# State-space scans with interleaved convolution layers on one core: decays computed three states ahead, statistics deferred behind the next product

## The chip, the cores and the metric

The kernel runs on one core of one Trainium2 chip. A core has five engines that each work through their own queue in order: TensorE (PE in the profile; PEld are its weight loads), VectorE (DVE), ScalarE (ACT), GpSimd (POOL) and SyncE (SP), which here only issues DMA transfers. They meet through semaphores. The metric is the device time of one execution in microseconds (us); the time before is the median of three runs.

## The reference, cut to what matters

The input x is 16 images of 192 channels of 64 x 64. Four layers follow, each `x = x + layer(group_norm(x))`:

- layer 0: a small per-channel network (1-3-3-3-1, with tanh) at x - 0.5 and x + 0.5, then the absolute difference of two sigmoids;
- layer 1: a linear map over the channels of a pixel and its four neighbours;
- layer 2: a selective scan, which takes most of the time (below);
- layer 3: depthwise 3x3, 5x5, 1x7 and 7x1 convolutions, a pointwise convolution, a batch norm over all images, a clip to [0, 6].

```python
# layer 2: K = 4 directions, N = 16 states, L = 4096 positions
xs = jnp.stack([xf, xt, xf[..., ::-1], xt[..., ::-1]], axis=1)   # rows, columns, both backward
dts, Bs, Cs = jnp.split(jnp.einsum('bkdl,kcd->bkcl', xs, x_proj_weight), [R, R + N], axis=2)
delta = softplus(einsum('bkrl,kdr->bkdl', dts, dt_projs_weight) + dt_projs_bias)
A = -exp(A_logs)
def step(h, inp):
    d, u, Bt, Ct = inp
    dA = exp(d[..., None] * A)
    h = dA * h + (d * u)[..., None] * Bt[:, :, None, :]
    return (h, einsum('bkdn,bkn->bkd', h, Ct))
```

The sums over n are added over the four directions, with a skip term. The group norms need the mean and variance of each layer's input: these are the statistics of which the change speaks.

## The kernel before

**Tiling.** Images are worked in 8 pairs; a pair's 2 x 192 channels make three blocks j of 128 partitions. For one pair `scans` (L761) does layer 2 and `layer3` (L1018) layer 3. The layers 0 and 1 and the projections that feed layer 2 are the generator `front` (L359); while pair i is scanned, the front of pair i + 1 is worked a little at a time between the scan's steps. The front of the first pair runs alone ahead of everything, with three interleaved streams of layer 0 (`deep`). The eighth pair has no front beside it.

**A scan step.** `todo` holds 48 tiles (j, direction, chunk of 1024 positions), each with 16 states n: 768 steps s a pair, 6144 in all. A step takes

- `load_c` (L829): SP loads a row of C, broadcast to 128 partitions, into `cb` (4 buffers), two steps ahead;
- `spread` (L875): two matmuls put B of state n on all partitions, into PSUM `pbt` (2 buffers), two steps ahead;
- `decay` (L868): ScalarE makes `dA = exp(delta * a)`, into `dA` (2 buffers), two steps ahead;
- `product` (L888): VectorE multiplies `pbt` by `du` in place;
- `scan` (L891): VectorE's scan `h = dA * h + pbt` along the positions (8 buffers `h`), then ScalarE's copy of the last column into `state`, then GpSimd's `h * cb`, and for every fourth step a DMA that adds one `h` to another;
- `add_up` (L909): TensorE sums the `h` of a tile in PSUM `ysum`, four steps behind; ScalarE copies the result to `X` or `Xt` (L939).

At n = 3 of each tile `step_rest` (L845) makes the next tile's `delta` by a softplus, for which ScalarE loads another table, and loads it back for the next decay.

**What sets the order.** Inside `scans` every engine call is kept in the order in which the program makes it (`_InOrder`, L54). So the loop at L970 is the order by hand: `load_c(s + 2)`, `product(s)`, `scan(s)`, `decay(s + 2)`, `spread(s + 2)`, then the parts of n = 3 and 8, then one slot of the front, then `add_up(s - 4)`. During layer 0 a step has one slot of the front, at n = 0 two and at n = 3 and 5 none (L1003); elsewhere about one, two where n is a multiple of 4, and matmuls of layer 1 count as half a slot.

**Statistics on VectorE.** `bn_stats` works on 512 columns (0.67 to 0.69 us each). It stands in the front for the input (L385, two a slot), for the result of layer 0 (L490, in `tail`, L464) and of layer 1 (L626, in `done`, L620), and in `finish` (L941) for X, the sum of both scan orientations, when a block j is done. `finish` adds `Xt` to `X` on GpSimd (on VectorE for the last block) in four chunks, one a step from n = 5, with the statistics of each chunk one step later. Since slots come after `scan(s)`, all these statistics stand behind a scan and ahead of the next product.

**Layer 0's order.** A chunk of x is 128 x 512; it has four units q of four slots each. `tail` goes on by one yield a slot: GpSimd and ScalarE turn the network's output into a likelihood, GpSimd adds it to x (L487), and two yields later come the statistics and the store of x (L490, L491). The load of the chunk two ahead (L548) stands in the second slot of q = 3 and takes the buffer (of 3) that the tail has just left. `norm` (L427) of the next chunk is in the second slot of q = 1.

Of the kernel before, what the change touches and what calls it, by code (L numbers as in the profile page):

```python
# [11 lines left out]
F32 = mybir.dt.float32  # L12
# [10 lines left out]
P = 128  # L23
# [45 lines left out]
class _Engines:  # L69
# [3 lines left out]
    def __init__(self, tc, in_order):  # L73
        nc = tc.nc
        of = (lambda e: _InOrder(tc, e)) if in_order else (lambda e: e)
        self.pe, self.act, self.dve = of(nc.tensor), of(nc.scalar), of(nc.vector)
        self.gps, self.sp = of(nc.gpsimd), of(nc.sync)
        self._in_order, self._table = in_order, None

    def table(self, *names):  # L80
# [11 lines left out]
def conv_preact_kernel(ctx: ExitStack, tc: tile.TileContext, a: dict):  # L92
# [266 lines left out]
    def front(i, o, E, ps, deep):  # L359

        with tc.tile_pool(name="f_st", bufs=1) as stat:
# [4 lines left out]
            with tc.tile_pool(name="f0", bufs=3) as pool:  # L366
# [12 lines left out]
                for u in range(4 * NT):  # L379
                    yield  # L380
                    load(u + 2)
                    j, c = divmod(u, 4)
                    x = got.pop(u)
                    for h in range(2):
                        E.dve.bn_stats(sts[0][:, j, 2 * c + h, :], x[:, 512 * h : 512 * h + 512])  # L385
            yield
# [11 lines left out]
    def layer0(i, E, ps, deep, st, gm, rstd):  # L398
        with tc.tile_pool(name="l0w", bufs=1) as w_, tc.tile_pool(name="l0x", bufs=3) as xk, tc.tile_pool(
# [11 lines left out]
            def stream(chunks, no):  # L411
# [52 lines left out]
                def tail(ci):  # L464
# [21 lines left out]
                    E.gps.tensor_scalar(sg, sg, 1e-6, None, ALU.max)  # L486
                    E.gps.tensor_tensor(x, x, sg, ALU.add)  # L487
                    yield
                    yield
                    E.dve.bn_stats(st[:, j, c, :], x)  # L490
                    E.sp.dma_start(out=row_tiles(x1_d)[:, j, 512 * c : 512 * c + 512], in_=x)  # L491

# [34 lines left out]
                for u, (ci, q) in enumerate(units):  # L527
# [17 lines left out]
                    if q == 1:  # L545
                        norm(at + 1)
                    if q == 3:
                        load(at + 2)  # L548
                        xns.pop(ci)
                    yield "l0"  # L550

                    for s in (1, 0):
# [3 lines left out]
                        first(u + 1, s)  # L556
                        tanh(t2[:, s, :], ba[s][:GR], 2, g, s)
                        yield "l0"
                    before = ci, q, g, ba, t2
# [19 lines left out]
    def layer1(o, E, ps, deep, st, gm, rstd):  # L579
        with tc.tile_pool(name="l1w", bufs=1) as w_, tc.tile_pool(name="l1x", bufs=2) as xk, tc.tile_pool(  # L580
# [39 lines left out]
            def done(c, jo, p):  # L620
# [4 lines left out]
                yield  # L625
                E.dve.bn_stats(st[:, jo, c, :], x)  # L626
                E.sp.dma_start(out=row_tiles(o.x2)[:, jo, 512 * c : 512 * c + 512], in_=x)

            def advance():
# [131 lines left out]
    def scans(i, o, st3, nxt):  # L761

        E = _Engines(tc, True)
        with ExitStack() as es:
# [5 lines left out]
            two = pool("l2two", 2)  # L770
            hp = pool("l2h", 8)
            cp = pool("l2c", 4)
            sp_ = pool("l2s", 3)
# [94 lines left out]
            def decay(s):  # L868
                t, n = divmod(s, N)
                j, k, at, first = todo[t]  # L870
                dA = dAs[s] = two.tile([P, LC], F32, name="dA")
                E.table(TANH)
                E.act.activation(dA, made[t][0], AF.Exp, scale=a_neg[:, k, j, n : n + 1])
# [67 lines left out]
            def finish(j):  # L941

                for c in range(4):
# [5 lines left out]
                    yield  # L949
                    for h in range(2 * c, 2 * c + 2):  # L950
                        E.dve.bn_stats(st3[:, j, h, :], X[:, 512 * h : 512 * h + 512])
                yield
# [6 lines left out]
            for _ in step_rest(0):  # L959
                pass  # L960
            load_dt(1)
            for s in range(2):
                load_c(s)
                decay(s)
                spread(s)
# [4 lines left out]
            for s in range(total):  # L970
# [8 lines left out]
                if n == 6:  # L979
                    load_xc(t + 1)  # L980
                product(s)
                scan(s)
                if s + 2 < total:
                    decay(s + 2)
                    spread(s + 2)
# [16 lines left out]
                if kind == "l0":  # L1002
                    for _ in range({0: 2, 3: 0, 5: 0}.get(n, 1)):  # L1003
                        kind = next(fr, None) if kind == "l0" else kind
                elif n not in (3, 5):
                    done = 0
# [7 lines left out]
            for g in (finish(NT - 1), fr):  # L1014
                for _ in g:
                    pass

# [286 lines left out]
```

## Time and profile before

| what | value |
|---|---|
| median of 3 runs | 28522.85 us (28516.71 to 28527.12) |
| the profiled execution: its own time | 28505.5 us |
| its span, first to last instruction | 28503.4 us |
| VectorE busy | 24241.3 us (85%) |
| TensorE busy / weight loads | 23450.2 us (82%) / 9578.6 us (34%) |
| GpSimd busy | 20851.6 us (73%) |
| ScalarE busy | 16193.3 us (57%) |
| DMA | 191 GB/s on the mean |
| granted TensorE clock | 0.909 on the mean |
| scans (VectorE), 6144 | 2.35 us each with a state, 2.29 without |
| products (VectorE), 6144 | 1.21 us each |
| decays (ScalarE), 6144 | 1.15 us each |
| h times cb (GpSimd), 6144 | 2.45 us each |

Busy is the time in which an engine has an instruction in work. Idle time of an engine is listed with what ended it, which is inferred from the semaphores: `DVE h L64 <- ACT dA L64` is VectorE's scan (it writes `h`) that waits for ScalarE's decay. L64 is the line of the recording helper, so instructions inside `scans` are told apart by their tiles, not by their lines. A few of VectorE's waits are large but lie outside the scans: `fst L490` and `l_xr L624` in the first pair's front, `l_p` in layer 3, `rl` in the last pass.

### The profile page before, as it was taken

To read this page: it belongs to the slowest core of one execution; us is meant where nothing else is said; L and a number is where in the kernel's file an instruction comes from. 1 tells how busy PE (TensorE), PEld (TensorE's weight loads), DVE (VectorE), ACT (ScalarE), POOL (GpSimd) and SP (SyncE) were. 2 spreads that over 40 slices of the span, in tenths; PEclk is the share of its full clock that TensorE was granted. 3 is DMA by queue.
4 is the path that set the end of the run, shared out by engine and by line. 5 is a ranking of instruction groups with operands and counts; after the bars stand their busy time and mean duration, and the time that the engine had idled before them with its cause. 6 is when DMAs were issued, how large, how long until landed. Compare 5 with 4: busy or idle time off the path is not lost. (4 is left out here: it accounts for less than half of the span.)

```text
span 28503.4 us, 207850 instructions
## 1 busy us (share of the span) xinstructions
PE 23450.2 (82%) x57140; PEld 9578.6 (34%) x57140; DVE 24241.3 (85%) x15397; ACT 16193.3 (57%) x23037; POOL 20851.6 (73%) x10440
## 2 busy tenths in 40 slices
PE   8799977999689987899879997799968998766663
PEld 4333323333233332333323332333323333222221
DVE  0388988899889988989888898888988988899994
ACT  7377445774467643775447744577445764344443
POOL 2388876887768876788768887688776887777772
PEclk9899988999899998999889998899989999888886
DMA  4478864887568974788747887478855887467765
GB/s 101 133 215 214 213 200 137 215 211 214 162 175 220 215 214 118 215 214 216 210 124 214 215 214 205 132 216 213 216 170 166 217 210 218 121 187 190 190 184 234
DMA packets 2007999, 5447.98 MB, mean 191 GB/s; under 512 B 550392, under 2 KB 550616, under 8 KB 1989424
## 3 DMA queue, kind: packets, MB, share of 16 engines
q1 hardware_dynamic: 1782192, 4578.95, 55.6%
q0 software_dynamic: 221184, 805.40, 14.9%
q10 hardware_dynamic: 3456, 50.33, 0.4%
q8 instruction: 455, 7.45, 0.1%
q14 instruction: 712, 5.83, 0.1%
HBM read 3896.19 MB, written 329.51 MB: 148 GB/s over the span
## 5 line engine op out<-in xcount | busy, mean ns | idle before, releaser
L64 POOL TENSOR_TENSOR h<-h,cb 128x1024 f32<-128x1024 f32 x6144 | 14820.0, 2447 | 4719.8 <-ACT state L64 4189.9
L64 DVE TENSOR_TENSOR_SCAN h<-dA,state,pbt 128x1024 f32<-128x1024 f32 x4608 | 10813.8, 2347 | 1135.7 <-ACT dA L64 614.9
L64 PE MATMUL ysum<-h,ident 128*128 128x512 f32 x18432 | 9406.9, 635 | 45.8 <-DMA h<-h 45.5
L64 DVE TENSOR_TENSOR pbt<-du,pbt 128x1024 f32<-128x1024 f32 x6144 | 7429.5, 1209 | 377.1 <-PE pbt L64 341.4
L64 ACT ACTIVATE dA<-delta,t_alog 128x1024 f32<-128x1024 f32 x6144 | 7035.5, 1146 | 6.6
L64 PEld LDWEIGHTS ysum<-h,ident 128*128 128x128 f32 x18432 | 3764.6, 205 | 4305.5 <-issue 3922.7
L64 ACT COPY state<-h 128x1 f32<-128x1 f32 x6144 | 1150.0, 187 | 6955.5 <-DVE h L64 6903.8
L64 PE MATMUL pbt<-bp,pick 96*128 96x512 bf16 x8192 | 2716.5, 416 | 2246.5 <-DVE h L64 2216.1
L64 DVE TENSOR_TENSOR_SCAN h<-dA,pbt 128x1024 f32<-128x1024 f32 x1536 | 3512.4, 2287 | 362.7 <-ACT dA L64 152.8
L64 PE MATMUL p<-t,wts 96*128 96x512 f32 x5376 | 2741.3, 610 | 136.0 <-ACT t L64 136.0
L64 PE MATMUL p<-m,wms 128*96 128x512 f32 (+1 forms) x5376 | 2724.3, 609 | 10.5 <-ACT lu L64 10.0
L64 ACT ACTIVATE t<-p,bias 96x512 f32<-96x512 f32 x2688 | 1814.2, 680 | 1104.1 <-PE p L64 1095.4
L64 PEld LDWEIGHTS <-pick 96*128 96x128 bf16 x8192 | 692.3, 101 | 5114.8 <-DVE h L64 3431.4
L1071 POOL TENSOR_TENSOR l_g<-l_g,l_m 128x1024 f32<-128x1024 f32 x672 | 1614.8, 2405 | 454.8 <-ACT l_g L1067 348.2
L64 PE MATMUL l_p<-l_xp,w1s 128*128 128x512 f32 x3920 | 1851.4, 604 | 7.0 <-POOL l_xp L64 7.0
L64 PE MATMUL pbt<-bp,pick_mix 96*128 96x512 bf16 x4096 | 1307.4, 402 | 634.0 <-DVE h L64 620.2
L1094 DVE SCALAR_TENSOR_TENSOR l_p<-xp,wc,l_p 128x1024 f32<-128x1024 f32 x1248 | 1589.6, 1287 | 257.4 <-PE l_p L1088 226.5
L64 POOL DMA_DIRECT2D h<-h x1536 | 1355.0, 882 | 494.9 <-POOL h L64 426.3
L1076 PE MATMUL l_p<-xp,diag 128*128 128x512 f32 x2688 | 1286.0, 637 | 333.0 <-DVE l_y L1094 281.2
L64 PEld LDWEIGHTS p<-t,wts 96*128 96x128 f32 x5376 | 1024.6, 193 | 1295.7 <-issue 882.7
L64 ACT ACT_TABLE_LOAD x1104 | 1416.4, 1283 | 19.5
L64 POOL TENSOR_TENSOR du<-delta,xn 128x1024 f32<-128x1024 f32 x384 | 1022.7, 2663 | 451.4 <-ACT delta L64 451.4
(219 smaller groups left out, 17750.1 us busy)
## 6 DMA issues: line engine op xcount, KB each, us to landing
cb<-cp_d SPq DMA_DIRECT2D x2048, 512.0 KB
cb<-c_d SPq DMA_DIRECT2D x2048, 512.0 KB
h<-h POOLq DMA_DIRECT2D x1536, 512.0 KB, 6.9
cb<-cp_d SPq DMA_DIRECT2D x2048, 256.0 KB
cb<-c_d SPq DMA_DIRECT2D x2048, 256.0 KB
m<-l_xn SPq DMA_DIRECT2D x3072, 128.0 KB
bp<-bp_d SPq DMA_DIRECT2D x384, 192.0 KB
f0x<-in_x SPq DMA_DIRECT2D x96, 512.0 KB
```

Of the source, the lines that this page charges most:

```text
L64: return self._tc.keep_in_program_order(call(*args, **kw))
L1071: nc.gpsimd.tensor_tensor(g, g, m, ALU.add)
L1076: nc.tensor.matmul(ps[:, cs], diag[:, j, t, :], window(j, 16 * c + 8 * h, 8, tap), start=(t == 0), stop=False,)
L1094: nc.vector.scalar_tensor_tensor(image(y if tap is TAPS[-1] else ps), window(j, 16 * c, 16, tap), factor(j, tap), image(ps), ALU.mult, ALU ...
```

## The change

Two things change, both in the order of the program.

1. `dA` gets a pool of its own with three buffers, and decays are issued three steps ahead: decay(s + 3) where decay(s + 2) stood. Spreads and loads of C stay two ahead.
2. Statistics of the in-order front and of `finish` are not issued at once but collected (`later`) and issued by `between`, which the loop calls after `product(s)` and ahead of `scan(s)`; in layer 0's slots of n = 0 and n = 12 it is also called directly behind the slot. The tails of layer 0 and layer 1 get a yield: layer 0's statistics and store come three yields after the addition instead of two, and both tails end one yield later. `finish` has two yields a chunk instead of one. Layer 0's load of the chunk two ahead goes from the second slot of q = 3 to the fourth. In the first pair's front and in layer 3, which are not kept in order, `later` issues at once.

No computation is added or taken away.

```diff
+    def later(self, call):
+        if self._in_order:
+            self._later.append(call)
+        else:
+            call()
+
+    def between(self):
+        for call in self._later:
+            call()
+        self._later.clear()
...
                     x = got.pop(u)
-                    for h in range(2):
-                        E.dve.bn_stats(sts[0][:, j, 2 * c + h, :], x[:, 512 * h : 512 * h + 512])
+                    def stats(x=x, j=j, c=c):
+                        for h in range(2):
+                            E.dve.bn_stats(
+                                sts[0][:, j, 2 * c + h, :], x[:, 512 * h : 512 * h + 512]
+                            )
+                    E.later(stats)
...
                     E.gps.tensor_tensor(x, x, sg, ALU.add)
-                    yield
-                    yield
-                    E.dve.bn_stats(st[:, j, c, :], x)
+                    for _ in range(3):
+                        yield
+                    E.later(lambda: E.dve.bn_stats(st[:, j, c, :], x))
                     E.sp.dma_start(out=row_tiles(x1_d)[:, j, 512 * c : 512 * c + 512], in_=x)
+                    yield
...
                     if q == 1:
                         norm(at + 1)
-                    if q == 3:
-                        load(at + 2)
-                        xns.pop(ci)
                     yield "l0"
...
                         tanh(t2[:, s, :], ba[s][:GR], 2, g, s)
+                        if q == 3 and s == 0:
+                            load(at + 2)
+                            xns.pop(ci)
                         yield "l0"
...
-                E.dve.bn_stats(st[:, jo, c, :], x)
+                E.later(lambda: E.dve.bn_stats(st[:, jo, c, :], x))
                 E.sp.dma_start(out=row_tiles(o.x2)[:, jo, 512 * c : 512 * c + 512], in_=x)
+                yield
...
+            da = pool("l2a", 3)
...
-                dA = dAs[s] = two.tile([P, LC], F32, name="dA")
+                dA = dAs[s] = da.tile([P, LC], F32, name="dA")
...
                     yield
-                    for h in range(2 * c, 2 * c + 2):
-                        E.dve.bn_stats(st3[:, j, h, :], X[:, 512 * h : 512 * h + 512])
+                    yield
+                    def stats(c=c):
+                        for h in range(2 * c, 2 * c + 2):
+                            E.dve.bn_stats(st3[:, j, h, :], X[:, 512 * h : 512 * h + 512])
+                    E.later(stats)
...
+            for s in range(3):
+                decay(s)
             for s in range(2):
                 load_c(s)
-                decay(s)
                 spread(s)
...
                 product(s)
+                E.between()
                 scan(s)
+                if s + 3 < total:
+                    decay(s + 3)
                 if s + 2 < total:
-                    decay(s + 2)
                     spread(s + 2)
...
                         kind = next(fr, None) if kind == "l0" else kind
+                        if n in (0, 12):
+                            E.between()
...
             for g in (finish(NT - 1), fr):
                 for _ in g:
-                    pass
+                    E.between()
+            E.between()
```

More of the change, by code (lines that the diff above doesn't have):

```diff
@@ L77, in __init__ @@
         self.gps, self.sp = of(nc.gpsimd), of(nc.sync)
+        self._later = []
         self._in_order, self._table = in_order, None
+    def later(self, call):
[7 more added lines that the diff above has]
+        self._later.clear()
     def table(self, *names):
@@ L487, in tail @@
                     E.gps.tensor_tensor(x, x, sg, ALU.add)
+                    for _ in range(3):
+                        yield
+                    E.later(lambda: E.dve.bn_stats(st[:, j, c, :], x))
+                    E.sp.dma_start(out=row_tiles(x1_d)[:, j, 512 * c : 512 * c + 512], in_=x)
                     yield
-                    yield
-                    E.dve.bn_stats(st[:, j, c, :], x)
-                    E.sp.dma_start(out=row_tiles(x1_d)[:, j, 512 * c : 512 * c + 512], in_=x)
                 def advance():
```

## The prediction

> **What bounds the kernel now.** I read the page's shares first: VectorE is busy 24241.3 us of a 28503.4 us span and has the largest share, so what counts is the 4262 us in which it idles. Then the windows of two pairs of images, from the first scan to the last: the seventh, which carries the front (layers 0, 1 and the projections) of the next pair in its slots, and the eighth, which carries none. Columns: window, length, busy time of PE, PEld, DVE, ACT, POOL, granted clock, DMA share, GB/s.
>
> ```profile
> 21577.20:24615.00 3037.80, 2633.98 (x6528) 1079.29 (x6528) 2754.52 (x1681) 1888.02 (x2753) 2375.91 (x1187) 0.93 0.80 211
> 24974.80:27775.00 2800.20, 1928.03 (x4204) 716.39 (x4204) 2671.57 (x1553) 1166.65 (x1722) 2119.53 (x1014) 0.83 0.69 189
> ```
>
> VectorE paces both: idle 283.3 us with a front, 128.6 without. So a front causes 154.7 us of idling a pair, 1083 us over the seven pairs that have one: a ceiling for a change that only removes idle time. Next, VectorE's waits (total us, times, longest), the rows that lie in the scans:
>
> ```profile
> DVE h L64 <- ACT dA L64: 767.7, 937, 4.5
> ...
> DVE pbt L64 <- PE pbt L64: 341.4, 428, 5.9
> ...
> DVE fst L64 <- POOL l_x L64: 125.3, 71, 4.2
> ...
> DVE st L64 <- POOL X L64: 103.3, 57, 5.6
> ```
>
> The first row is scans waiting for their decay; the third and fourth are statistics waiting for GpSimd; the second is products waiting for TensorE's spread, which the change does not touch. The timelines of VectorE and ScalarE around step n=3 of a tile of 16 steps show how a decay comes late (start, length, instruction, idle time):
>
> ```profile
> 12295.57 1.21 DVE L64 TENSOR_TENSOR pbt<-du,pbt 128x1024 f32<-128x1024 f32 x1
> 12296.88 2.35 DVE L64 TENSOR_TENSOR_SCAN h<-dA,state,pbt 128x1024 f32<-128x1024 f32 x1
> 12299.14 1.21 DVE L64 TENSOR_TENSOR pbt<-du,pbt 128x1024 f32<-128x1024 f32 x1
> 12301.99 2.35 DVE L64 TENSOR_TENSOR_SCAN h<-dA,state,pbt 128x1024 f32<-128x1024 f32 x1 [1.64 <-ACT dA L64]
> ```
>
> ```profile
> 12295.92 1.01 ACT L64 COPY X<-ysum 128x1024 f32<-128x1024 f32 x1 [1.92 <-PE ysum L64]
> 12296.95 1.28 ACT L64 ACT_TABLE_LOAD   x1
> 12298.25 1.11 ACT L64 ACTIVATE delta<-v,t_dtb 128x1024 f32<-128x1024 f32 x1
> 12299.26 0.18 ACT L64 COPY state<-h 128x1 f32<-128x1 f32 x1
> 12299.46 1.28 ACT L64 ACT_TABLE_LOAD   x1
> 12300.76 1.15 ACT L64 ACTIVATE dA<-delta,t_alog 128x1024 f32<-128x1024 f32 x1
> ```
>
> Product to scan is 1.31 us from start to start, scan to product 2.26: a step of 3.57. The scan at 12301.99 is n=6; it could have begun at 12299.14 + 1.31 = 12300.45. Its decay waited on ScalarE behind the copy of the sums, the softplus and two table loads.
>
> **Part A, decays three ahead.** No instruction is added. Each decay moves one step forward in ScalarE's order and still waits, through the state copy ahead of it, for the scan that frees its buffer. So decay s now ends where decay s-1 ended, and its slack grows by 3.57. Before, it had 1.31 + 2.26 + 1.31 = 4.88 us from the end of scan s-2, and needs 0.19 + 1.15, so a ScalarE lag over 3.5 us showed; after, over 7.1.
> The 767.7 us are not all real. In 513 waits the scan starts within 0.13 us of its own decay's end and more than 0.06 us past the nominal 1.31; they hold 709 us. The rest are gaps of about 0.2 us with the decay long done, at one scan in four, which waits for four semaphores; they stay.
> Not all of the 709 is won. Spreads stay two ahead in two PSUM buffers, in TensorE's queue behind matmuls that need ScalarE's tanh, so a late ScalarE also makes the next spreads late. At 12801.58 a scan (n=3) starts 3.21 us late for a decay; the spread two steps on ends at about 12807.6, and its product starts there: that wait would only move. I therefore bounded each of the 513 waits by the smallest spare time (product's start less the end of its spread) of the steps behind it, up to the first spread that began within 0.25 us of the scan that released it, since from there TensorE follows VectorE. Whole trace, by position, waits / covered in us: n=6 379.0 / 270.6; n=3 97.9 / 25.1; n=7 64.8 / 60.4; n=4 44.7 / 7.4; n=11 31.2 / 31.2; n=15 28.2 / 0.9; n=5 23.2 / 0.5; the others 40.2 / 16.0. Sum 709 / 412. I take **412**; ends 271 (n=6 alone) and 709 (TensorE's queue moves forward too). What is late next is the spread.
>
> **Part B, statistics a slot later.** Layer 0's wait for x (125.3 us, longest 4.2): the statistics come a slot later and mostly behind one more product, 3.57 + 1.2 = 4.8 us, beyond the longest wait. 28 of 168 stay directly behind a scan, so **115**; ends 0 and 125. The statistics of X (103.3 us): their additions go from steps 5, 6, 7, 8 to 5, 7, 9, 11 and the statistics to 8, 10, 12, 14, so 8.4 us instead of 3.6 behind the addition; but in those tiles GpSimd is nearly as full as VectorE (59.5 and 60.4 us busy in the tile from 12405 to 12480), so it may not catch up: **60**; ends 0 and 103.
>
> **Part C, statistics between a product and its scan.** This row shows both effects:
>
> ```profile
> 12278.43 2.35 DVE L64 TENSOR_TENSOR_SCAN h<-dA,state,pbt 128x1024 f32<-128x1024 f32 x1
> 12280.70 0.67 DVE L64 BATCH_NORM_STATS2 fst<-l_x 128x6 f32<-128x512 f32 x1
> 12281.28 1.21 DVE L64 TENSOR_TENSOR pbt<-du,pbt 128x1024 f32<-128x1024 f32 x1
> 12282.59 2.35 DVE L64 TENSOR_TENSOR_SCAN h<-dA,state,pbt 128x1024 f32<-128x1024 f32 x1
> ```
>
> Instructions that don't depend on each other start 0.08 to 0.09 us before the one ahead ends (scan to statistics 2.27 for 2.35, statistics to product 0.58 for 0.67); scan on product, which depends, starts 0.10 after its end. No row has statistics straight behind a product they don't need; by the others it would be 1.21 - 0.09 = 1.12, then 0.60 to the scan: 1.72 where now 0.60 + 1.31 = 1.91 are spent. In the changed order 442 groups stand so (168 of layer 1, 140 of layer 0, 70 of the input, 64 of X): 442 x 0.19 = **84**; ends 44 (the 0.10 gap alone) and 84. No product behind statistics has under 0.65 us to spare on its spread, so 0.6 us earlier costs none of them a wait.
> [...]
>
> **What else moves.** Layer 0's load of x goes two slots later, still six slots (over 20 us) ahead of its normalisation; nothing of VectorE waits for it now. On SP it no longer stands right behind the store of the same buffer, where SP waited 650.6 us for landings; the broadcast rows (cb) queue behind it, but only GpSimd waits for them (187.7 us with c_d), which is not the bound: 0. Stores of x come a slot later too: 0. Layer 0 gets one slot longer; the front is done some seven tiles ahead of the pair's end, which covers 3.6 us. The first front is scheduled freely and only its load and tail move: 0, at worst one of its slots, about 6 us.
>
> **The sum.** 412 + 115 + 60 + 84 = 671 us. The profiled execution took 28505.5 (span 28503.4), which gives 27834; it lies 17 us under the median of the runs, 28522.85, so on that scale **27850**. All high ends: 709 + 125 + 103 + 84 = 1021, or 27500, close to the ceiling of 1083. All low ends: 271 + 44 = 315, or 28210.
>
> **Rivals.**
> 1. *The spread takes over (18%).* ScalarE's lag stays what it is, so TensorE's queue is late in more places, and GpSimd's statistics waits return where VectorE runs ahead. For it: products already wait 341.4 us for spreads. Against: at n=6, over half of the waits, the spare time is there. Only the low ends remain: about 28210.
> 2. *TensorE's queue moves forward too (10%).* My spare times treat a spread that is behind tanh as fixed; if it gains with VectorE, nearly every wait goes: about 27500.
> 3. *TensorE becomes the bound by its clock (6%), slower than before.* In a tile with layer 0 its records cover 58 of some 61 us, and a matmul that takes 0.59 at full clock takes 1.06 at the lower one. If denser work lowered the granted clock, 0.93 in the seventh pair, its 2634 us of a pair would stretch by 2634 x (0.93 / c - 1). With half of the stretch falling through to VectorE, the gain of 96 us a pair is eaten at c = 0.87; at 0.85 it is 124 a pair, 28 x 7 = 200 us slower, 28720. Against: the eighth pair has less matmul work and a lower clock, 0.83.
> 4. *It does nothing (4%):* decays would still end late because each waits for the scan that frees its buffer. Against: that scan is now three back. 28520.
>
> **Chances.** The forecast has 62%, the rivals 18, 10, 6 and 4. Faster by over 0.2%, about what a measurement of this kernel can tell from no change: 0.62 + 0.18 + 0.10 = 0.90; the same 0.04; slower 0.06. The range takes in rivals 1 and 2 with the ends of the unknown costs: 27480 to 28230.
>
> **What would show it.** Right for A: scans' wait for dA falls from 768 to below 300 us, nothing left at n=6, and products' wait for pbt grows from 341 to some 600. Right for B: both statistics rows below 60 us together. Right for C: product to scan 1.7 us where statistics stand between. Wrong: waits for dA as before (A does nothing), the pbt row above 900 (rival 1), or a granted clock below 0.87 in the pairs with a front (rival 3). The eighth pair should hardly change, 2800 us.

## The result, and the profile after

Median of 4 runs 28274.64 us (28253.27 to 28295.17), the kernel before beside it 28519.78 (28509.89 to 28527.12): ratio **0.9914**, 95% interval 0.9897 to 0.9931. Faster by 245 us, where 671 were forecast; the time lies just above the range, whose upper end was 28230. The profiled execution took 28295.17, its span is 28293.1 and its mean clock 0.904 (before 0.909).

The windows of the seventh and eighth pair, first scan to last, columns as before:

```profile
21391.40:24394.70 3003.30, 2639.30 (x6528) 1088.12 (x6528) 2751.99 (x1681) 1873.26 (x2754) 2374.57 (x1189) 0.93 0.81 214
24764.20:27554.60 2790.40, 1931.18 (x4204) 718.63 (x4204) 2670.79 (x1553) 1165.90 (x1722) 2119.14 (x1016) 0.83 0.69 190
```

VectorE's busy time is within 3 us of before in both pairs. The pair with a front lost 34.5 us (3037.8 to 3003.3), the one without 9.8. The granted clock of these two windows is 0.93 and 0.83, to two digits as before. VectorE's waits (total us, times, longest):

```profile
DVE pbt L64 <- PE pbt L64: 812.1, 862, 9.7
...
DVE h L64 <- ACT dA L64: 116.8, 512, 2.3
DVE st L64 <- POOL X L64: 115.6, 44, 4.1
...
DVE fst L64 <- POOL l_x L64: 3.6, 7, 0.5
```

Scans hardly wait for late decays any more (767.7 to 116.8, and 476 of the 512 waits left are gaps of at most 0.3 us), nor statistics for x (125.3 to 3.6). But products wait 812.1 us for spreads where 341.4 stood and some 600 were expected, and the statistics of X wait no less than they did (103.3 to 115.6). The step that the prediction showed, scan n=6 of the same tile, now looks so; first VectorE, then ScalarE, then TensorE:

```profile
12193.02 2.35 DVE L64 TENSOR_TENSOR_SCAN h<-dA,state,pbt 128x1024 f32<-128x1024 f32 x1
12195.73 1.23 DVE L64 TENSOR_TENSOR pbt<-du,pbt 128x1024 f32<-128x1024 f32 x1 [0.37 <-PE pbt L64]
12197.17 2.35 DVE L64 TENSOR_TENSOR_SCAN h<-dA,state,pbt 128x1024 f32<-128x1024 f32 x1 [0.20 <-DVE pbt L64]
```

```profile
12192.65 1.01 ACT L64 COPY X<-ysum 128x1024 f32<-128x1024 f32 x1 [1.92 <-PE ysum L64]
```

```profile
12193.71 1.13 PE L64 MATMUL v<-dt,t_dtw 12*128 12x512 f32 x4 [1.10 <-ACT X L64]
12194.77 0.92 PE L64 MATMUL pbt<-bp,pick 96*128 96x512 bf16 x2
12195.49 3.30 PE L64 MATMUL p<-m,wms 128*96 128x512 f32 x4
```

The scan that stood 1.64 us for its decay has it in time. Now its product stands 0.37 for the spread, which stands in TensorE's queue behind the matmuls of `v`; these need the PSUM banks of `ysum`, and so ScalarE's copy of the sums. Here 1.64 became 0.57 (0.37 and 0.20).

Part C did what it was to do. VectorE with a statistic between product and scan:

```profile
12239.68 1.21 DVE L64 TENSOR_TENSOR pbt<-du,pbt 128x1024 f32<-128x1024 f32 x1
12240.80 0.68 DVE L64 BATCH_NORM_STATS2 fst<-l_x 128x6 f32<-128x512 f32 x1
12242.17 2.35 DVE L64 TENSOR_TENSOR_SCAN h<-dA,state,pbt 128x1024 f32<-128x1024 f32 x1 [0.68 <-DMA h<-h]
```

The statistic starts 1.12 after the product, as worked out (this scan then waits for another thing). Over the trace, with layer 0's 140: product to statistic 1.116, statistic to scan 0.600, together 1.716 in the median. Before, a statistic of layer 0 and then product to scan took 1.90 in the median of the 97 groups in which nothing waited (0.585 and 1.315), so the place is worth 0.185 us, as forecast. The Trainium skill's page "VectorE: DVE Perf Modes", section "The DRAIN you can't avoid", says that an instruction does not start until the pipe is empty behind the one ahead, and adds that one that is not held starts earlier. This trace agrees with the addition: the statistic, which needs nothing of the product, starts 0.09 us before the product's end (1.12 for 1.21).

### The profile page after: what moved, and what is told of

It reads as the page before. It is cut to its first block, busy times and chain, and to the rows that moved or that the text cites. A ratio compares the mean times of both kernels' runs of the same rounds, so it can differ in the third digit from the quotient of the medians.

```text
span 28293.1 us, 208020 instructions
## 1 busy us (share of the span) xinstructions
PE 23483.5 (83%) x57140; PEld 9639.0 (34%) x57140; DVE 24223.9 (86%) x15397; ACT 16092.7 (57%) x23037; POOL 20787.2 (73%) x10440
## 5 line engine op out<-in xcount | busy, mean ns | idle before, releaser
L64 DVE TENSOR_TENSOR pbt<-du,pbt 128x1024 f32<-128x1024 f32 x6144 | 7441.2, 1211 | 852.4 <-PE pbt L64 812.1
```

Source lines behind the costliest of these rows:

```text
L64: return self._tc.keep_in_program_order(call(*args, **kw))
```

## The experiments: what each part is worth

Each kernel's ratio is against runs of the kernel before on the same chip (median 28528 to 28536; 28520 beside the changed kernel), with its interval; differences between kernels are those of their medians, unless a ratio is named. Where the chips differ, so can the medians by these 16 us. Three theories were open when the first four ran: Q, that a late ScalarE makes TensorE's queue late and so the spreads; S, that the statistics' new place holds back what follows the scan; G, that GpSimd's lag reaches the spreads by way of the sums of h.

**e1, the decays alone.** The kernel before, `dA` in its own pool of three, decays three ahead.

```diff
+            da = pool("l2a", 3)
...
-                dA = dAs[s] = two.tile([P, LC], F32, name="dA")
+                dA = dAs[s] = da.tile([P, LC], F32, name="dA")
...
+                if s + 3 < total:
+                    decay(s + 3)
                 if s + 2 < total:
-                    decay(s + 2)
                     spread(s + 2)
```

> The kernel before with part A alone: three buffers for dA and decays three ahead, statistics where they were. Theory Q (a late ScalarE makes TensorE's queue late through the tanh and the copy of the sums, so the spread takes over the wait): scans' wait for dA under 150 us, products' wait for pbt from 341 to 650 or more, the time 150 to 300 us under before, so 28220 to 28370. Rival S (the statistics' new place in front of the scan holds back the scan's followers and eats part A's gain): part A alone wins over 400 us, under 28120. Rival G (GpSimd's lag, through the sums of h, is what makes the spreads late): as Q in time, but TensorE's idle ahead of late spreads is put down to h and its DMA.

28525.07, ratio 0.9994 (0.9986 to 1.0003): no gain at all, where Q expected at least 150 us and S over 400. The rows are Q's: scans' wait for decays 767.7 to 125.4, products' for spreads 341.4 to 705.0. And the statistics of x wait 240.0 instead of 125.3; that such waits return where VectorE runs ahead stood in the prediction's first rival.

**e2, the statistics alone** (the changed kernel, decays two ahead, the pool with two buffers).

```diff
-            da = pool("l2a", 3)
+            da = pool("l2a", 2)
...
-                if s + 3 < total:
-                    decay(s + 3)
+                if s + 2 < total:
+                    decay(s + 2)
                 if s + 2 < total:
```

> The changed kernel without part A: two buffers for dA, decays two ahead; statistics deferred, a slot later, load of x later. Theory Q: the waits for GpSimd's x (125 us) go, product to scan with statistics between is 0.19 us shorter in 442 places, but VectorE meets the decays earlier: 50 to 200 us under before, 28320 to 28470, with scans' wait for dA above 768. Rival S: no gain or slower, 28500 or more.

28422.67, ratio 0.9958 (0.9945 to 0.9970). Spreads 343.6, decays 837.4: the spreads get late only with part A, and the statistics alone win time, so S falls.

**e3, part C alone** (e2 without the added slots of part B).

```diff
-                    for _ in range(3):
+                    for _ in range(2):
                         yield
                     E.later(lambda: E.dve.bn_stats(st[:, j, c, :], x))
...
-                    yield
                     def stats(c=c):
```

> Part C alone: statistics between product and scan, with layer 0's and X's statistics at the old number of yields and decays two ahead (layer 0's load of x stays at its later place, the end of the tails too). Theory Q: 30 to 90 us under before, 28430 to 28490; the difference to the run with deferred statistics a slot later is what the later slot (part B) is worth. If the pipe empties whatever the order, part C is worth nothing: within 30 us of before, if GpSimd's waits are as before.

28433.85, ratio 0.9965 (0.9951 to 0.9978): all but some 11 us of e2. A statistic behind the next product is already 1.2 us later: the wait for x falls from 125.3 to 69.5 by that alone. Part B's added slots (e3 to e2) take another 69 us from x's row and 10 from X's, yet they are worth only those 11 us: scans wait longer for decays instead, first e3, then e2.

```profile
DVE h L64 <- ACT dA L64: 774.5, 941, 3.9
```

```profile
DVE h L64 <- ACT dA L64: 837.4, 939, 9.2
```

In all three one row had grown that has nothing to do with scans: VectorE's additions of X at the end of a pair waited 119 us for ScalarE's copy, for 54.9 before. The gaps between the last scan of one pair and the first of the next had gone from 2519.9 to 2565.0 us in all (after against before). GpSimd shows why; before, then after, at the end of the same pair:

```profile
14433.36 1.20 POOL L1040 TENSOR_SCALAR diag<-ident,wc 128x128 f32<-128x128 f32 x2 [1.09 <-DVE h L64]
14434.53 2.35 POOL L64 TENSOR_TENSOR h<-h,cb 128x1024 f32<-128x1024 f32 x1
```

```profile
14296.73 8.72 POOL L1073 TENSOR_SCALAR diag<-ident,wc 128x128 f32<-128x128 f32 x15
14305.42 2.34 POOL L64 TENSOR_TENSOR h<-h,cb 128x1024 f32<-128x1024 f32 x1
```

The instructions that build layer 3's weights are not kept in order. With the new pool 15 of them, not 2, stand ahead of the pair's last `h * cb`, on which its last sums, the copy of X and layer 3 wait. Two kernels test it.

**e5, the changed kernel with the old pool.**

```diff
-            da = pool("l2a", 3)
...
-                dA = dAs[s] = da.tile([P, LC], F32, name="dA")
+                dA = dAs[s] = two.tile([P, LC], F32, name="dA", bufs=3)
```

> The changed kernel whole, but the three decay buffers taken from the pool that held the two before (bufs=3 on that one tile) instead of from a pool of their own. Theory P (the new pool costs time between pairs): with the pool, 15 of the 21 instructions that build layer 3's diagonal weights stand ahead of GpSimd's last product h x cb of each pair; with the old pool 2 do. 13 x 0.6 us = 7.8 us later for the last sums, of which 6.4 us a pair showed (gaps between pairs 2565 us in all against 2520 before, end 738 against 728), so this kernel should take 55 us less than the changed one, about 28220, with VectorE's wait for ScalarE's X at the pair's end back from 119 to some 55 us. Rival: the gaps grew because the additions of X and their statistics come later; then nothing changes, 28275. The waits within the scans (decay 117, spread 812) should be as in the changed kernel by both.

**e6, the kernel before with the pool alone.**

```diff
+            da = pool("l2a", 2)
...
-                dA = dAs[s] = two.tile([P, LC], F32, name="dA")
+                dA = dAs[s] = da.tile([P, LC], F32, name="dA")
```

> The kernel before, with nothing changed but that its two decay buffers come from a pool of their own. Theory P: 50 to 55 us slower than before, about 28585, gaps between pairs 2565 instead of 2520, the wait for ScalarE's X 119 instead of 55, and every wait within the scans as before (decay 768, spread 341). Rival: no difference, 28530.

e5: 28208.34, ratio 0.9886 (0.9873 to 0.9900), 66 us under the changed kernel. e6: 28606.62, ratio 1.0025 (1.0015 to 1.0035), 71 us over the kernel before. The additions' wait for X in e5 and in e6 (54.9 before, 118.8 in the changed kernel):

```profile
DVE X L64 <- ACT X L64: 54.5, 8, 6.8
```

```profile
DVE X L64 <- ACT X L64: 119.4, 8, 15.0
```

The pool's price is shown from both sides; the gaps between pairs sum to 2507.1 and 2569.0 us.

**e15, the decays alone in the old pool** (the kernel before).

```diff
-                dA = dAs[s] = two.tile([P, LC], F32, name="dA")
+                dA = dAs[s] = two.tile([P, LC], F32, name="dA", bufs=3)
...
+                if s + 3 < total:
+                    decay(s + 3)
                 if s + 2 < total:
-                    decay(s + 2)
                     spread(s + 2)
```

> The kernel before with the decays three ahead alone, in the old pool: e1 without the pool's price of 67 to 71 us. By theory P 28455 (e1 28525 less 70), so that this part is worth some 75 us in place of the 412 forecast; the decays' row falls to about 125 and the spreads' grows to about 705, as in e1. If it stays at 28520, the pool's price is not what hid this part in e1.

28452.72, ratio 0.9971 (0.9960 to 0.9983): 76 us, as expected. VectorE's waits in it:

```profile
DVE pbt L64 <- PE pbt L64: 764.2, 754, 7.8
...
DVE fst L64 <- POOL l_x L64: 252.3, 110, 4.5
...
DVE h L64 <- ACT dA L64: 125.8, 526, 1.1
DVE h L64 <- DVE pbt L64: 123.0, 592, 0.6
...
DVE h L64 <- ACT state L64: 35.8, 93, 2.9
```

Two rows of the kernel before that were not shown yet:

```profile
DVE h L64 <- ACT state L64: 120.4, 153, 4.3
...
DVE h L64 <- DVE pbt L64: 69.2, 335, 0.6
```

The first of them is a row of late decays too: in 114.5 of its 120.4 us the scan starts within 0.13 us of the end of its own decay, and the list names the state copy of another step, which stands directly behind that decay in ScalarE's order and which the scan does not need (e4, below, 485.9 of 512.2; e16 176.0 of 180.6).

Against before: decays -642, state copies -85; spreads +423, statistics of x +127, the small gaps of scans behind their product +54. Of 727 us taken away 604 stand elsewhere in the same list.

So the gain of 245 is made up, by the ratios (after 0.86%, e2 0.42%, e6 0.25%, of 28520): B and C 191 (e2's 120 and the pool's 71), A on top of them 125 (e2 to after), the pool -71. In the other order A is worth 76 (e15), and B and C on top of it 240: the parts are not independent of each other.

## The experiments: what holds the spreads

**e4, the changed kernel with decay(s + 3) at the end of the step**, behind the front's slot and `step_rest`, so that the tanh and the copy of the sums go ahead of it.

```diff
-                if s + 3 < total:
-                    decay(s + 3)
                 if s + 2 < total:
                     spread(s + 2)
...
                             E.between()
+                if s + 3 < total:
+                    decay(s + 3)
```

> The changed kernel with decay(s + 3) issued at the end of the step, behind the front's slot and the parts of n = 3, instead of right behind the state copy. The tanh and the copy of the sums come up to 1.15 us earlier on ScalarE, and the decay has slack to spare. Theory Q: products' wait for pbt falls from 812 to 650 us or less and the time lies 80 to 250 us under the changed kernel, 28020 to 28190, with scans' wait for dA under 250. Rival G: products' wait for pbt stays within 60 us of 812, and the time within 40 us of the changed kernel's 28275.

28556.25, ratio 1.0006 (0.9997 to 1.0014). VectorE's waits:

```profile
DVE h L64 <- ACT state L64: 512.2, 382, 7.9
DVE pbt L64 <- PE pbt L64: 350.8, 455, 5.7
DVE h L64 <- ACT dA L64: 337.7, 553, 3.6
```

The spreads' row fell, as Q has it and G has not. But the time is far from what Q expected: scans wait for late decays again, 850 us by the two rows, nearly as in the kernel before (888). ScalarE's last idle time ahead of these waits stands at the copy of the sums for 401 of the 850 us and at a tanh of layer 0 for 158, both waiting for TensorE. So the fallen row alone does not speak against G: a scan that is held up hides a late spread, as in the kernel before. ScalarE's order decides who waits, VectorE's product or its scan.

**e7, no table loads for delta** (the changed kernel, exp in place of softplus, which computes another delta).

```diff
-                E.table(SOFTPLUS)
-                E.act.activation(delta, v, AF.Softplus, bias=dtb[:, k, j : j + 1])
+                E.table(TANH)
+                E.act.activation(delta, v, AF.Exp, bias=dtb[:, k, j : j + 1])
```

> The changed kernel with delta = exp(v + b) in place of softplus(v + b), a change of what is computed: the exponential's table is the decays' own, so two table loads of 1.28 us go from ScalarE at each step n=3. It tells what makes the spreads late. Theory Q (ScalarE's lump at n=3 makes TensorE's queue late, by the front's tanh and by the matmuls of v): of the 812 us that products wait for spreads, 447 us lie at n=5 to 8, behind a lump of about 5 us of which 2.6 us go; the waits fall to 450 to 600 and the time to 27950 to 28100. Rival G (the spreads are late because TensorE's own queue is too full around them, or because of GpSimd): the row stays above 740 and the time within 60 us of the changed kernel.

28230.74, ratio 0.9894 (0.9880 to 0.9907), 44 us under the changed kernel. ScalarE's table loads in the scans, after and e7:

```profile
L64 ACT ACT_TABLE_LOAD x1104 | 1416.4, 1283 | 19.3
```

```profile
L64 ACT ACT_TABLE_LOAD x344 | 441.4, 1283 | 6.1
```

975 us of ScalarE's work went and the spreads' row fell from 812 to 790. Q in this form, ScalarE's lump at n=3, falls; the row and the time are what G expected. At n=6 nothing could change, in fact (163 and 159 us): the matmuls of `v` wait for the copy, which is ahead of the table load.

**e8, `v` behind the spread for n=6.**

```diff
-                    gstep = step_rest(t + 1) if t + 1 < T else iter(())
-                    next(gstep, None)
+                elif n == 4:
+                    gstep = step_rest(t + 1) if t + 1 < T else iter(())
+                    next(gstep, None)
                 elif n == 8:
```

> The changed kernel with the next tile's step (matmuls of v, softplus) one step later, at n=4 and so behind the spread for n=6 in TensorE's queue; v takes the PSUM banks that the copy of the sums must have emptied. Theory V (the spread for n=6 is late because it stands behind the matmuls of v, which wait for ScalarE's copy of X or Xt; in the changed kernel 250 of the 812 us have that wait as TensorE's last idle time): the waits at n=6 fall from 163 to below 60 us. The first sums of the tile, at n=5, then wait for the softplus in the same banks, and the spread for n=8 behind them: if that gives it all back, n=7 and 8 grow from 201 to over 300 and the time is 28275 or more; if TensorE has the time to spare there, 28130 to 28220. Rival: n=6 stays above 130, because the spread is held by the front's matmuls, and the time within 40 us.

28148.40, ratio 0.9867 (0.9851 to 0.9882), 126 us under the changed kernel. TensorE at the same step:

```profile
12111.99 0.60 PE L64 MATMUL pbt<-bp,pick 96*128 96x512 bf16 x2
12113.25 1.13 PE L64 MATMUL v<-dt,t_dtw 12*128 12x512 f32 x4 [0.67 <-ACT X L64]
12114.31 1.96 PE L64 MATMUL p<-m,wms 128*96 128x512 f32 x4
```

The wait for the copy is still there, but the spread for n=6 is past it. Late spreads at n=6 go from 163 us to none, those at n=7 and 8 stay (201 and 198 together). The row is 618.3.

**e9, e8 in the old pool.**

```diff
-                dA = dAs[s] = da.tile([P, LC], F32, name="dA")
+                dA = dAs[s] = two.tile([P, LC], F32, name="dA", bufs=3)
```

> The changed kernel with both edits that won alone: decay buffers in the old pool (67 us, between pairs) and the matmuls of v behind the spread for n=6 (126 us, within the scans). They lie in different stages, so if the two explanations hold they add up: 28075 to 28090. If less than 150 us of the 193 remain, one of them takes from the other.

28099.90, ratio 0.9845 (0.9832 to 0.9859), 175 under the changed kernel: 49 more than e8 (63 by the ratios), where 67 were expected. The two add up within what the medians can tell.

**e10, no wait for t1** (e9; the result of layer 0 is another one).

```diff
-                        add(ba[s], wt[:, g, :P], t1[:, s, :])
+                        add(ba[s], wt[:, g, :P], m0[:GR, s, :])
```

> e9 with one matmul of layer 0 fed other data: the one that adds t1, the tanh that ScalarE made in the slot ahead, reads m0 instead, so that TensorE no longer waits for that tanh (the tanh is still computed; what layer 0 computes is another thing). Theory T: in e8 162 of 618 us of late spreads stand behind that wait, so they go: products' wait for spreads falls to 440 to 500 and the time is 120 to 160 us under e9. Rival: TensorE then waits in the next matmul for something as late (t2, or the copy of the sums), the row falls by less than 60 us and the time by less than 50.

28088.58, ratio 0.9840 (0.9826 to 0.9853): 11 us, within what can't be told from e9. The groups by shape show that I had the wrong tanh. What is left of `p<-t` is the closing matmul, and all of the idle time is before it:

```profile
L64 PE MATMUL p<-m,wts 96*128 96x512 f32 x2688 | 1393.2, 599 | 0.0
L64 PE MATMUL p<-t,wts 96*128 96x512 f32 x2688 | 1354.1, 620 | 152.4 <-ACT t L64 152.2
```

**e13, no wait for t2** (e9; the result of layer 0 is another one).

```diff
-                        tanh(t2[:, s, :], ba[s][:GR], 2, g, s)
+                        tanh(t2[:, s, :], m0[:GR, s, :], 2, g, s)
...
-                    before = ci, q, g, ba, t2
+                    before = ci, q, g, ba, t1
```

> e9 with layer 0's last tanh taken off TensorE's path: the closing matmul reads t1 instead of t2, and the tanh that makes t2 reads m0 instead of the bank (as many instructions on each engine, another result of layer 0). e10 took t1's wait away and 176 us of late spreads behind "ACT t" stayed, so they can only be the wait for t2, made by the last instruction of the slot before. Theory T: they go, the products' wait for spreads falls from 638 to 460-500 us and the time to 27920-27980. Rival: TensorE is late there for want of its own time and finds the next wait at once; the row stays above 580 and the time above 28050.

28002.82, ratio 0.9813 (0.9800 to 0.9827): 97 us under e9, between the two expectations. The spreads' row falls by 116, and part of the wait comes back one matmul later, where TensorE waits for ScalarE's copy out of the same bank (90.6 us, for 13.6 in e9):

```profile
L64 PE MATMUL p<-t,wts 96*128 96x512 f32 x5376 | 2677.9, 601 | 0.0
...
L64 PE MATMUL p<-m,wms 128*96 128x512 f32 x2688 | 1299.4, 606 | 90.6 <-ACT lu L64 90.0
```

**e11, the projections normalised a chunk ahead** (e9, three buffers).

```diff
-                    xns[c] = xk.tile([P, NT, 512], F32, name="pj_x")
+                    xns[c] = xk.tile([P, NT, 512], F32, name="pj_x", bufs=3)
...
+                    norm(c + 1, at)
                     r = xk.tile([P, 512], F32, name="pj_r", tag="pj_r")[:m]
...
+                    yield 0.36
```

> e9 with the projections' normalisation (ScalarE) of chunk c+1 put between the matmul groups of chunk c, in three buffers instead of two, so that TensorE finds each normalised chunk ready. In e8 128 us of the late spreads have the wait of pj_p for pj_x ahead of them, in two tiles of 48. Theory T: these go, the row falls by 100 to 130 and the time is 90 to 130 us under e9. Rival: the load is only moved, ScalarE is full there and its decays or r copies get late instead: less than 40 us.

28020.66, ratio 0.9818 (0.9805 to 0.9832): 79 under e9; the spreads' row 638 to 490, but scans wait 197 us instead of 143 for the DMAs that add up h.

**e12, the double slot at n=10** (e9).

```diff
-                    for _ in range({0: 2, 3: 0, 5: 0}.get(n, 1)):
+                    for _ in range({3: 0, 5: 0, 10: 2}.get(n, 1)):
...
-                        if n in (0, 12):
+                        if n in (10, 12):
```

> e9 with the front's two slots in one step of a tile moved from n=0 to n=10. In e8 the late spreads behind tanh lie at n=4 and 5 (100 of 162 us), some steps behind the double slot at n=0, and few at n=9 to 11. If the double slot makes ScalarE late there, the row falls by 60 to 100 us and the time by as much. Rival: the lateness at n=4 and 5 is that of the sums' copy at n=3 alone; then it stays and n=12 to 14 grow, so that the time is the same or up to 60 us longer than e9.

28012.29, ratio 0.9815 (0.9801 to 0.9828): 88 under e9. Late spreads behind a tanh at n=4 and 5 fall from 123 to 30 us, while those at n=1 and 2 grow from 0 to 44 and those at n=13 from 18 to 49; with other links, n=13 grows from 29 to 113. The statistics of x, which no longer go ahead at n=0, wait 79.8 us instead of 4.2 (85.4 in e14, below).

**e14, e11 with e12's edit.**

```diff
-                    for _ in range({0: 2, 3: 0, 5: 0}.get(n, 1)):
+                    for _ in range({3: 0, 5: 0, 10: 2}.get(n, 1)):
...
-                        if n in (0, 12):
+                        if n in (10, 12):
```

> e9 with both of e11 (projections normalised a chunk ahead; 79 us under e9) and e12 (double slot at n=10; 88 us under e9): both take late spreads away, in different tiles for the most part, though the projections' waits fell in e12 too (129 to 88). If they add, 27933; if they share, 27960 to 27990. Not faster than either: over 28010.

**27977.38**, ratio 0.9805 (0.9792 to 0.9819), the fastest of this study: 297 us under the changed kernel. The two edits share part of their gain (123 of 167).

**e16, e14 with the decays two ahead.**

```diff
-                if s + 3 < total:
-                    decay(s + 3)
                 if s + 2 < total:
+                    decay(s + 2)
                     spread(s + 2)
```

> e14 with the decays two ahead again. Theory: what took the gain of the third decay is that the spreads stand in TensorE's queue behind matmuls that wait for ScalarE; with three of those waits relieved (v, projections, double slot) the third decay is worth more than in the kernel before: 150 to 300 us over e14. Rival: the third decay is worth what it was, 75 to 110 us, since a scan can be no earlier than its spread wherever ScalarE is late.

28025.46, ratio 0.9821 (0.9808 to 0.9835): the third decay is worth 48 us there, less than before. The theory falls, and the rival (75 to 110) put it too high. VectorE's waits in e16, then in e14:

```profile
DVE h L64 <- ACT dA L64: 364.6, 668, 3.5
DVE pbt L64 <- PE pbt L64: 293.2, 428, 4.1
...
DVE h L64 <- ACT state L64: 180.6, 86, 8.4
```

```profile
DVE pbt L64 <- PE pbt L64: 522.3, 618, 7.5
...
DVE h L64 <- ACT dA L64: 109.0, 505, 0.6
```

The third decay takes 256 from the decays' row and 164 from the state copies', and gives 229 to the spreads, as everywhere. And the edits that relieve TensorE had already relieved the scans: with decays two ahead, they wait for decays 545 us by the two rows here, 888 in the kernel before.

**e17 and e18, less work for TensorE** (e14 and e16 without the matmul that adds t1, so without a part of layer 0).

```diff
-                        add(ba[s], wt[:, g, :P], t1[:, s, :])
```

> e14 without the matmuls of layer 0 that add t1 (1344 in the scans, by e14's rows 1.01 us of TensorE each, 7.5 us a tile with layer 0; part of layer 0 is left out). e10 has shown that their wait for the tanh is worth nothing, so what this takes away is TensorE's time. In e14 a tile with layer 0 takes 60.8 us, TensorE covers 57.6 of it and VectorE 56.3; tiles without a front take 57.8. Theory F (in tiles with layer 0 TensorE is the fuller engine, and its fullness holds the spreads): these tiles fall to 58.0 to 59.5 us, the time by 230 to 500 us, to 27480 to 27750, and the spreads' row from 522 to under 350. Rival L (ScalarE's lag paces TensorE and VectorE alike): its order and work are unchanged, so the time is within 100 us of e14.

> e17 with the decays two ahead again; against e17 it gives what the third decay is worth when TensorE has time to spare. Theory F: more than the 48 us it is worth in the pair e14, e16 and the 76 us in e15: 120 us or more, since the decays' waits that remain (255 us above the floor in e16) have no late spread to change into. Rival L: 30 to 80 us as before.

28017.17 and 28035.74, ratios 0.9822 (0.9808 to 0.9835) and 0.9829 (0.9815 to 0.9842). e17 is 40 us slower than e14: the first pair's front, which is scheduled anew, takes 43 us longer (1214 to 1257), and the scans of the seven pairs are the same within 16 us (20716.5 and 20731.7). The spreads' row is 552.2 where F expected under 350. The third decay is worth 19 us, where F expected 120 or more and L 30 to 80. The seventh pair's tiles with layer 0 in e14 and e17:

```profile
21250.00:22832.60 1582.60, 1499.34 (x3806) 618.74 (x3805) 1464.11 (x866) 1254.54 (x1853) 1327.91 (x671) 0.98 0.87 221
```

```profile
21294.30:22887.60 1593.30, 1413.30 (x3426) 561.03 (x3425) 1463.01 (x866) 1256.76 (x1852) 1326.58 (x671) 0.94 0.87 219
```

TensorE is less busy by 86 us of 1499 and the stretch is no shorter. Theory F falls too: 86 us less of TensorE's work a pair do not make the spreads earlier.

What stands: in these tiles no engine is busy all the time (TensorE 95%, VectorE 93% of e14's stretch above), and work taken from ScalarE (975 us) or TensorE (86 a pair) is worth 44 us or nothing, while links between their two queues are worth 126 (v), 97 (t2), 79 (projections) and 88 (where two slots meet). Spreads and decays hang on the same two queues, and the waits that come from them, for spreads and for decays (the latter in two rows, decays and state copies), change into each other:

| kernel | spreads | decays | state copies | sum | time |
|---|---|---|---|---|---|
| before | 341 | 768 | 120 | 1229 | 28520 to 28536 |
| e15, A alone | 764 | 126 | 36 | 926 | 28452.7 |
| after | 812 | 117 | 15 | 944 | 28274.6 |
| e4, decays behind the front | 351 | 338 | 512 | 1201 | 28556.3 |
| e9 | 638 | 112 | 6 | 756 | 28099.9 |
| e14 | 522 | 109 | 17 | 648 | 27977.4 |
| e16, e14 without A | 293 | 365 | 181 | 839 | 28025.5 |

How the 423 us of new late spreads in e15 divide can be read from TensorE's last idle time ahead of each late spread (before, then e15): at the matmuls of `v` 107 to 305 us, at layer 0's tanh 35 to 137, at the projections 147 to 199, at the sums of h, G's way, 10 to 53. So G has a small part of it. Open is what each link costs in time: relieving one moves some of its wait to the next (e13's 90 us, e12's n=13), so the gains measured one by one don't add up to the row.

## Why the prediction was wrong

- **What bounds the kernel:** right. VectorE's idle time in pairs with a front is where the gain came from, and the eighth pair hardly changed (2800.2 to 2790.4).
- **Part A, the step that failed:** 412 us forecast, 125 measured in the full change and 76 alone (e15). The decays' row fell as said, and at n=6 the cover rule held: decays' wait 357 to 6 us, spreads' 73 to 163. It failed over the rest of the tile. The rule followed a wait to the first spread on VectorE's heels, "since from there TensorE follows VectorE". It doesn't: a VectorE that is 2 or 3 us earlier meets the next link of the two queues that has a time of its own. Spreads got late at n=8 (58 to 124), 5 (17 to 83), 0 (12 to 70), 12 (9 to 71), of which the rule had priced only a part: the row rose by 468 (e2 to after), where 709 - 412 = 297 was allowed. And scans that come earlier find the DMA sums (+43) and their product (+57) a little late, too.
- **A reading in part A:** the 709 us were taken as a part of the decays' row of 767.7. Of these waits 101 us stand in the row of the state copies (120.4), which the prediction did not show. So some 160 us of the decays' row were small gaps, not 59, and most of the 116.8 that are left are such gaps.
- **Part B:** x's row fell as forecast (115, though 140/168 of the row is 104; 122 went, about half of it by part C's displacement). That a row's fall is time won was wrong here too: the added slots alone took 79 us from the two rows and won 11 (e3 to e2), since scans then waited 63 longer for decays. What they are worth with part A in place was not run. X's term was wrong: 60 forecast, the row went from 103.3 to 115.6, although the statistics come a step or more later. The prediction named the doubt, GpSimd nearly as full as VectorE there, and took the middle; which of GpSimd's instructions is in the way was not tried.
- **Part C:** right in the size of one statistic, 1.72 us measured and forecast. In time it was not measured apart from the displacement of x's statistics: e3's 101 us and the pool's 71 hold both. With the pool's 71 added back, B and C together are 191; by terms, 259 less X's 60 is 199. That these agree is in part luck: C with the displacement won more than its terms, and B's slots less.
- **What else moves, 0:** wrong by 71. I looked at loads and stores, not at instructions that the scheduler places freely; the order of GpSimd's instructions at the pair's end could have been compared before any run.
- **Rivals:** the first one, that the spread takes over, is what happened. It had 18%; the pbt row of 812 lies between the 600 and the 900 given as signs. Its 28210 is close to the changed kernel without the pool's price (e5, 28208), but by luck: it had 271 for A, 44 for C and nothing for B, where 125 for A and 191 for B and C were measured. Rival 2 is excluded by the spreads' row, which grew, and rival 4 by the decays' row. Rival 3's clock did not come (0.93 in the seventh pair as before; 0.904 for 0.909 on the mean of the execution).

The sum: 125 + 191 - 71 = 245, where 412 + 259 = 671 was forecast.

## What to carry to other kernels

When two waits of one engine hang on the same late queues, taking one away shows the other; price it by the rows that may grow, all the way along the tile, and not by the spare time at the place itself. Look for the link, the instruction that a queue stands at, before taking work from an engine: here four links were worth 79 to 126 us each, and a thousand microseconds of ScalarE's work 44. A new pool or buffer can move instructions that nothing holds in order; compare every engine's order at the places where stages meet.

## What the runs showed of the hardware that I had not expected

- With 192 matmuls of 1.01 us (two records each) taken out of a pair's tiles with layer 0 (e17), TensorE was busy only 86 us less, not 194: the granted clock fell from 0.98 to 0.94 there, and the matmuls that stayed got longer. The closing ones, `p<-t,wts`, took 657 ns on the mean for 613 in e14, told apart by their order from those that were taken out, and the other two of layer 0, `p<-m,wms`, 616 for 599. A TensorE with more gaps was given a lower clock, as in the eighth pair without a front (0.83 beside 0.93). Rival 3 feared the opposite, a lower clock for denser work.
- The place of a short VectorE instruction is worth 0.185 us: between two that depend on each other it adds 0.40 (1.716 for 1.313), ahead of a product that does not need it 0.585.
